# Group normalisation folded into the attention weights, and two new shares for GpSimd

## The chip, the cores and the metric

The kernel runs on one core of one Trainium2 chip. A core has five engines with queues of their own: TensorE (PE in the profile; its weight loads are listed as PEld), VectorE (DVE), ScalarE (ACT), GpSimd (POOL) and SyncE (SP, which here only issues the transfers between HBM and the on-chip memory). Each engine works through its queue in order and waits on semaphores for the others. The metric is the device time of one execution in microseconds; smaller is better.

## The reference

Input x has the shape (8, 512, 48, 48): 8 samples b, 512 channels, L = 2304 positions. Two layers follow each other, both of the form x + f(groupnorm(x)) with 32 groups of 16 channels.

Layer 0 is causal linear attention with 8 heads of 64 channels:

```python
n = groupnorm(x)
q, k, v = Wq @ n + bq, Wk @ n + bk, Wv @ n + bv
Q, K = elu(q) + 1, elu(k) + 1
den = 1 / (sum_c Q * cumsum(K) + 1e-10)
x = x + den * causal(Q, K) @ v
```

Layer 1 cuts the 512 channels into 4 scales s of 128. Each scale adds the result of the one before to its input, runs a Mamba block (a short convolution, SiLU, a projection to step, B and C, and a scan with 256 channels times 16 states), and fuses input and output by a maximum and two sigmoid weights:

```python
delta = softplus(dt @ Wdt + bdt)
h[t] = exp(delta[t] * A) * h[t - 1] + delta[t] * xs[t] * B[t]
y[t] = sum_n h[t, n] * C[t, n] + xs[t] * D
```

All of it is float32.

## The kernel before

**Two pipelines in one program.** Positions are cut into chunks of LC = 384 columns, NC = 6 to a row. Attention works on parts (b, o), o being one of four groups of 128 output channels (two heads); a part has 6 chunks, so there are 32 parts and 192 attention chunks. The second layer works on jobs (b, s, chunk), also 192, of two streams (even and odd samples) that take turns every 6 jobs. A job is 8 slots; a slot s holds 16 states times 128 channels of the scan in a tile u of 128 x 4 x 385.

**What a slot does.** u starts as the product of B (broadcast) and dxr = delta * xs. Its first LC - TAIL columns are made on DVE (`product`, L890, from a copy Bp of B in PSUM that ACT makes for two slots at a time, `inputs`, L863), the last TAIL = 152 on POOL (`last_product`, L879). ACT makes four decays exp(dr * A) in PSUM banks (L900). DVE runs four scans over u (L910). POOL multiplies all of u by C (`weigh`, L923). TensorE sums over states into yp (`gather`, L937). There are five buffers for u; POOL makes the tail of slot k+2 in slot k.

**What sets the order.** Nothing is scheduled by a compiler: Python generators (`Task`) yield a due time in half slots and the banks they need, and `beside` steps all that are due while `slot(k)` writes the instructions of slot k; the order written is the order on each engine. `ahead` writes decays up to 3 ahead of the scans (5 in two places). Six PSUM banks are shared by decays and attention. A job is 16 halves; every attention chunk takes a place 16 halves after the one before (`times`), so that in the long middle of the run each job carries one attention chunk.

**Around the change.** `statistics(b)` has DVE take batch statistics of x (L253, 24 pieces a sample) and `group_norm` makes of them norm[:, 0] = 1/std and norm[:, 1] = -mean/std per channel. `fetch` loads a chunk of 128 x 4 x 384 (tile xn) one chunk ahead. In `chunk(m)`, if o is 0, four POOL instructions (L324) scale and shift that chunk and a store keeps it as xns; parts with o from 1 to 3 load xns. `project(0)`, (1), (2) make q, k, v (L300: 4 matmuls each), `feature` applies elu + 1 with the bias of the projection (L312, L313 on ACT; L359, L367 on DVE). Later in the chunk: den by three small matmuls (L405), two DVE instructions that add 1e-10 and take the reciprocal (L433, L434), a broadcast, and the scores and outputs. `load_projections` loads the weights of the next part at the last chunk but one of a part.

In `prepare`, a job goes through the convolution (L722), SiLU on ACT (L758 to L763, between two loads of activation tables), the projection to dt, B and C (L769, L774), the step size (L782 on PE, Softplus L793 on ACT with two more table loads), dx = delta * xs on POOL (L834, two), and the transfers that spread delta, dx, B and C over partitions. `pass_on` closes a block of 6 jobs and prepares the input of the next; its POOL addition L696 makes the output of the block before, one to a chunk.

Of the kernel before, what the change touches and what calls it, by code (L numbers as in the profile page):

```python
# [9 lines left out]
F32 = mybir.dt.float32  # L10
# [7 lines left out]
P = 128  # L18
T = 128
LC = 384  # L20
NI, NQ, NGR = 4, 4, 4
SLOTS = 8
TAIL = 152
BANKS = 6
# [25 lines left out]
def attention_then_mamba_kernel(  # L50
# [64 lines left out]
    def load_scales():  # L115
# [4 lines left out]
        nc.scalar.mul(w_a, w_a, -1.0)  # L120

    power = cpool.tile([P, 4], F32, name="power")
    nc.gpsimd.memset(power, -0.5)
# [98 lines left out]

    norms, xns, x1s, done, ksums = {}, {}, {}, {}, {}

    def statistics(b):

        xv = x[b].rearrange("(t p) l -> p t l", p=P)
        stats = small.tile([P, 4, NC, 6], F32, tag="stats_a", name=f"stats_a{b}", bufs=2)
        if b == 0:

            xs = []

            def load(c):
                t = mpool.tile([P, 4, 1 + LC], F32, tag="u", name=f"xs_{c}", bufs=5)[:, :, 0:LC]
                nc.sync.dma_start(out=t, in_=xv[:, :, c * LC : (c + 1) * LC])
                xs.append(t)

            for c in range(5):
                load(c)
            load_projections()  # L240
            for c in range(NC):
                for ct in range(4):
                    nc.vector.bn_stats(stats[:, ct, c, :], xs[c][:, ct, :])
                if c == 0:
                    load(5)
                    fetch(0)
        else:
            when = begins[b] + b % 2
            for i in range(4 * NC):
                yield (when - 4, 1) if b > 1 else "1", 0  # L250
                xs = piece(b, i)
                yield (when, 1) if b > 1 else "1", 0
                nc.vector.bn_stats(stats[:, i // NC, i % NC, :], xs)  # L253
                when += PERIOD
        norms[b] = yield from group_norm(stats, 4, f"a{b}", 2)
# [9 lines left out]
    def fetch(m):  # L265

        if m == len(parts):
            return
        b, o, c = parts[m]
        if (o, c) == (0, 0):  # L270
            xns[b] = dpool.tile([512, L], F32, tag="xn", name=f"xn_{b}", bufs=B)
            x1s[b] = dpool.tile([512, L], F32, tag="x1", name=f"x1_{b}", bufs=B)
        xn = apool.tile([P, 4, LC], F32, tag="xn", name=f"xn_{b}_{o}_{c}", bufs=2)
        src = (x[b] if o == 0 else xns[b]).rearrange("(t p) l -> p t l", p=P)
        nc.sync.dma_start(out=xn, in_=src[:, :, c * LC : (c + 1) * LC])
        fetched[m] = xn

    read, passes = [0], {}

    def chunk(m):  # L280
# [16 lines left out]
        def project(j):  # L297
            ps = bank()[:, 0:LC]
            for kt in range(4):
# [6 lines left out]
                )  # L306
            return ps, bqkv_sb[:, j * 4 + o : j * 4 + o + 1]

# [6 lines left out]

        if o == 0:
            yield at(-4), 0
            while b not in norms or m not in fetched:
                yield "1w", 0
            xn, norm = fetched.pop(m), norms[b]  # L320
            for ct in range(4):
                if ct:
                    yield at(ct - 4), 0
                nc.gpsimd.tensor_scalar(  # L324
                    xn[:, ct, :],
                    xn[:, ct, :],
                    norm[:, 0, ct : ct + 1],
                    norm[:, 1, ct : ct + 1],
                    ALU.mult,
                    ALU.add,  # L330
                )
            save(xns[b].rearrange("(t p) l -> p t l", p=P)[:, :, cols], xn)
        while read[0] < m - 1:
            yield "1w", 0
        yield at(0), 1
        if o:
            xn = fetched.pop(m)
        if c == 0:
# [22 lines left out]
        yield at(2, 0), 1  # L361
        kp, kb = project(1)
        yield at(3), 0
        ex = feature(kp, kb)
        yield at(4), 0
        k = new("k", 2)
# [19 lines left out]
        nc.vector.tensor_mul(pr, q, kc)  # L386
# [15 lines left out]
        both = bank()  # L402
        den = both[:, 0 : 2 * NT]
        for i in range(NT):
            nc.tensor.matmul(den[:, 2 * i : 2 * i + 2], pr[:, subs[i]], hsel, start=True, stop=True)  # L405
        more = NT if c + 1 < NC else NT - 1
# [25 lines left out]
        rd = small.tile([P, 2 * NT], F32, tag="rd", name=f"rd_{n}", bufs=1)  # L432
        nc.vector.tensor_scalar_add(rd, den, 1e-10)  # L433
        nc.vector.reciprocal(rd, rd)  # L434
        while read[0] < m:
# [86 lines left out]
    class Stream:  # L522
# [55 lines left out]
        def pass_on(self):  # L578
# [78 lines left out]
            for c in range(NC):  # L657
# [15 lines left out]
                else:  # L673
# [29 lines left out]
    class Job:  # L703
# [6 lines left out]
        def prepare(self):  # L710
# [66 lines left out]
            save(scr, dbc[0 : 2 * NS, :])  # L777
            yield "1", 2
            vps = []
            for h in range(2):  # L780
# [4 lines left out]
                vps.append(vp)  # L785
            while spreading:
                yield "1w", 0
# [72 lines left out]
        def inputs(self, pair):  # L860

            self.Bp = psx.tile([P, 2, LC - TAIL], F32, tag="Bp", name=f"Bp_{self.n}_{pair}")
            nc.scalar.copy(self.Bp, self.B[pair % 2][:, :, 0 : LC - TAIL])  # L863

# [7 lines left out]
        def last_product(self, s):  # L872

            shape, cols = [P, NGR, TAIL], slice(LC - TAIL, LC)
# [4 lines left out]
            nc.gpsimd.tensor_tensor(  # L879
                u[:, :, 1 + LC - TAIL :],  # L880
                self.B[q // 2][:, q % 2, cols].unsqueeze(1).to_broadcast(shape),
# [5 lines left out]
        def product(self, s, u):  # L887

            shape, cols = [P, NGR, LC - TAIL], slice(0, LC - TAIL)
            nc.vector.tensor_mul(  # L890
                u[:, :, 1 : 1 + LC - TAIL],
                self.Bp[:, s % 2, :].unsqueeze(1).to_broadcast(shape),
# [264 lines left out]
    def slot(k):  # L1157
# [9 lines left out]
        elif s == 6:  # L1167
            job.gated(0)
        beside(2 * k)
        for i in range(4):  # L1170
# [41 lines left out]
    with tc.manual_schedule():  # L1212
        half_no[0] = FIRST - 6
        Task(statistics(0)).finish()
        load_scales()
        for st in streams:
# [95 lines left out]
```

## Time and profile before

| what | us |
|---|---|
| median of 3 runs (8166.18 to 8179.68) | 8173.76 |
| the profiled execution, its own time | 8173.45 |
| its span, first to last instruction | 8171.6 |
| VectorE busy | 7825.8 |
| GpSimd busy | 7747.3 |
| TensorE busy (ends modelled) | 7371.7 |
| ScalarE busy | 6974.3 |
| first scan, last scan starts at | 196, 8145 |

The page's second part shows DVE and POOL at nine tenths or more in all of the 40 slices but the first. PE's granted clock is 0.945 of full speed on average. The transfers keep the 16 DMA engines busy to seven or eight tenths, at 203 GB/s. A duration in the group list is that of one instruction by itself; on DVE and POOL the next one starts somewhat before it ends, so what an instruction costs in a full queue is the distance from its start to the next start in the timeline.

### The profile page before, as it was taken

The numbers are of one execution on the slowest core, as the hardware profiler recorded it, in microseconds if no ns is written. First come the engines' busy times: TensorE is split into PE (matmuls) and PEld (weight loads), VectorE is DVE, ScalarE is ACT, GpSimd is POOL, SyncE is SP. The second block draws the span as 40 slices with busy tenths as digits, with TensorE's granted clock in tenths as the row PEclk, the third lists the DMA queues.
The fourth block names the chain that finished last, engine by engine and source line by source line (L and its number), as shares of the span: only waits on it lengthen the run. The fifth ranks groups of instructions, "written<-read, shape, count | busy, mean of one in ns | idle before, by whom it ended". The sixth has DMA issues, their size and how long they took to land. (4 is left out here: it accounts for less than half of the span.)

```text
span 8171.6 us, 133449 instructions
## 1 busy us (share of the span) xinstructions
PE 7371.7 (90%) x39882; PEld 3532.8 (43%) x39882; DVE 7825.8 (96%) x10534; ACT 6974.3 (85%) x14914; POOL 7747.3 (95%) x3905
## 2 busy tenths in 40 slices
PE   8889999998899999999899999999988999999975
PEld 5444444444444444444444444444444444444421
DVE  3999999999999999999999999999999999999998
ACT  3888888888888888888888888888888888888876
POOL 2999999999999999999999999999999999999999
PEclk9999999999999999999999999999999999999977
DMA  6778888877787788887787788887877777777765
GB/s 199 191 189 207 210 209 212 212 199 210 200 209 204 205 212 212 207 210 201 205 216 205 200 208 209 214 211 195 212 204 204 204 204 200 204 203 199 193 172 148
DMA packets 1097351, 1655.02 MB, mean 203 GB/s; under 512 B 143913, under 2 KB 989353, under 8 KB 1096498
## 3 DMA queue, kind: packets, MB, share of 16 engines
q1 hardware_dynamic: 1096626, 1646.48, 77.8%
q8 instruction: 317, 5.19, 0.3%
q14 instruction: 408, 3.34, 0.1%
HBM read 1318.23 MB, written 327.68 MB: 201 GB/s over the span
## 5 line engine op out<-in xcount | busy, mean ns | idle before, releaser
L910 DVE TENSOR_TENSOR_SCAN u<-bank,u 128x385 f32<-128x385 f32 (+1 forms) x6144 | 5435.3, 935 | 101.6 <-ACT bank L900 101.1
L923 POOL TENSOR_TENSOR u<-u,C 128x1536 f32<-128x1536 f32 x1536 | 4894.4, 3187 | 245.4 <-DVE u L910 164.3
L900 ACT ACTIVATE bank<-dr,scales 128x385 f32<-128x385 f32 (+1 forms) x6144 | 3422.3, 579 | 617.5 <-DVE u L910 573.9
L879 POOL TENSOR_TENSOR u<-B,dxr 128x608 f32<-128x608 f32 x1536 | 2285.6, 1488 | 14.8 <-DMA B<-scr 14.8
L300 PE MATMUL bank<-xn,wq 128*128 128x384 f32 x4608 | 1862.0, 552 | 262.4 <-DVE u L910 215.6
L890 DVE TENSOR_TENSOR u<-Bp,dxr 128x928 f32<-128x928 f32 x1536 | 1682.9, 1096 | 14.9 <-DMA dxr<-xscr 7.7
L937 PE MATMUL yp<-u,cst 128*32 128x384 f32 x12288 | 1357.6, 514 | 259.7 <-POOL u L923 147.7
L300 PEld LDWEIGHTS bank<-xn,wq 128*128 128x128 f32 x4608 | 939.9, 212 | 1153.2 <-DVE u L910 360.5
L722 PE MATMUL bank<-xi,wk 128*128 128x384 f32 x3072 | 1102.4, 502 | 14.5 <-ACT xr L508 13.7
L722 PEld LDWEIGHTS bank<-xi,wk 128*128 128x128 f32 x3072 | 556.2, 191 | 568.2 <-ACT bank L900 77.3
L937 PEld LDWEIGHTS yp<-u,cst 128*32 128x32 f32 x12288 | 249.3, 109 | 904.3 <-issue 412.7
L312 ACT ACTIVATE ex<-bank,bqkv_sb 128x384 f32<-128x384 f32 x384 | 221.1, 576 | 337.0 <-PE bank L300 336.1
L900 ACT ACT_TABLE_LOAD x382 | 490.1, 1283 | 6.9
L863 ACT COPY Bp<-B 128x464 f32<-128x464 f32 x768 | 419.6, 546 | 25.7 <-DMA B<-scr 12.4
L834 POOL TENSOR_TENSOR dx<-delta,xs 128x384 f32<-128x384 f32 x384 | 385.9, 1005 | 21.6 <-ACT delta L793 21.6
L733 PE MATMUL bank<-xi,scales 128*128 128x384 f32 x768 | 325.4, 510 | 50.3 <-ACT xs L758 50.3
L955 PE MATMUL bank<-yz,scales 128*128 128x384 f32 x768 | 328.1, 534 | 37.7 <-DVE yz L949 32.8
L782 PE MATMUL bank<-dbc,steps_w 9*128 9x384 f32 x768 | 306.0, 518 | 21.8 <-DVE rd L433 12.3
L769 PE MATMUL bank<-xs,scales 128*40 128x384 f32 x768 | 285.0, 494 | 0.0
L498 PE MATMUL bank<-sm,v 128*64 128x128 f32 x2304 | 255.2, 300 | 0.0
L793 ACT ACT_TABLE_LOAD x192 | 246.3, 1283 | 3.5
L758 ACT ACT_TABLE_LOAD x192 | 246.3, 1283 | 3.5
(123 smaller groups left out, 8101.2 us busy)
## 6 DMA issues: line engine op xcount, KB each, us to landing
dr<-dscr SPq DMA_DIRECT2D x1536, 192.0 KB, 4.2
dxr<-xscr SPq DMA_DIRECT2D x1536, 192.0 KB, 4.9
xn<-xn SPq DMA_DIRECT2D x192, 768.0 KB, 5.4
B<-scr SPq DMA_DIRECT2D x1536, 96.0 KB, 4.2
C<-scr SPq DMA_DIRECT2D x1536, 96.0 KB, 2.7
dscr<-delta SPq DMA_DIRECT2D x192, 384.0 KB, 5.2
xscr<-dx SPq DMA_DIRECT2D x192, 384.0 KB, 2.9
xn<-in_x SPq DMA_DIRECT2D x48, 768.0 KB, 5.3
```

The costliest lines, as they stand in the source:

```text
L300: nc.tensor.matmul(ps, wqs[m // NC][:, kt, j * P : (j + 1) * P], xn[:, kt, :], start=(kt == 0), stop=(kt == 3),)
L722: nc.tensor.matmul(xc, wk[:, k, h * P : (h + 1) * P], xi[:, c0 + k : c0 + k + LC], start=(k == 0), stop=(k == 3),)
L733: nc.tensor.matmul(zp, w_gate[:, s, h * P : (h + 1) * P], xi[:, c0 + 3 : c0 + 3 + LC], start=True, stop=True,)
L834: nc.gpsimd.tensor_tensor(dx[:, h, :], delta[:, h, :], xs[:, h, :], ALU.mult)
L863: nc.scalar.copy(self.Bp, self.B[pair % 2][:, :, 0 : LC - TAIL])
L879: nc.gpsimd.tensor_tensor(u[:, :, 1 + LC - TAIL :], self.B[q // 2][:, q % 2, cols].unsqueeze(1).to_broadcast(shape), self.dxr[h][:, :, col ...
L890: nc.vector.tensor_mul(u[:, :, 1 : 1 + LC - TAIL], self.Bp[:, s % 2, :].unsqueeze(1).to_broadcast(shape), self.dxr[s // NQ][:, :, cols],)
L900: nc.scalar.activation(dA[:, cols], self.dr[h][:, g, cols], AF.Exp, scale=w_a[:, self.w[1], NGR * h + g, q : q + 1],)
L910: nc.vector.tensor_tensor_scan(u[:, g, cols], dA[:, cols], u[:, g, cols], 0.0, ALU.mult, ALU.add,)
L923: nc.gpsimd.tensor_tensor(u[:, :, 0:LC], u[:, :, 1:], self.C[q // 2][:, q % 2, :].unsqueeze(1).to_broadcast([P, NGR, LC]), ALU.mult,)
L937: nc.tensor.matmul(self.yp[g * 32 : g * 32 + 32, 0:LC], state_sum, u[:, g, 0:LC], start=False, stop=s % NQ == NQ - 1, skip_group_check=True,)
L955: nc.tensor.matmul(self.xm[:, 0:LC], w_out[:, self.w[1], h, :], self.yz[:, h, :], start=(h == 0), stop=(h == 1),)
```

## The change

- The normalisation of attention's input leaves POOL. x itself is projected by every part; the weights are scaled by 1/std on ACT (`scaled`, four instructions of 128 x 384 a part, in place), and the shift goes into the bias: `shifts` multiplies the unscaled weights by -mean/std on PE (12 matmuls with one column a part, into three unused columns, 384 to 386, of the bank that holds k's projection), `shifted` adds the layer's bias on ACT (three instructions of 128 x 1). For the next part all this is done in the last chunk of the part before; for the first part in `adapt`, ahead of everything.
- The copy xns and its 48 stores are gone.
- The 1e-10 of the denominator comes from a matmul of the identity with a constant tile, ahead of the three of den; DVE takes the reciprocal straight from PSUM.
- POOL's share of the product is 128 columns in slots 0 and 1 of a job and 174 in slots 2 to 7.
- POOL's addition of `pass_on` moves to a place 17 halves ahead of the job (slot 7 in place of slot 4); the step-size matmuls L782 are written one half later, together with their Softplus; in slot 1 the gather that waits is written ahead of the other work.
- Statistics of samples 4 to 7 start earlier, with one piece every second job for each of two samples.

```diff
-TAIL = 152
+WIDE, TAIL = 128, 174
...
+    tiny = cpool.tile([P, 2 * LC // T], F32, name="tiny")
+    nc.gpsimd.memset(tiny, 1e-10)
...
-            when = begins[b] + b % 2
+            when, gap = begins[b] + (b % 2 if b < 4 else 0), PERIOD if b < 4 else 2 * PERIOD
...
-                when += PERIOD
+                when += gap
...
-        src = (x[b] if o == 0 else xns[b]).rearrange("(t p) l -> p t l", p=P)
+        src = x[b].rearrange("(t p) l -> p t l", p=P)
...
+    def shifts(i, to):
+        w, norm = wqs[i], norms[parts[i * NC][0]]
+        for j in range(3):
+            for kt in range(4):
+                nc.tensor.matmul(
+                    to[:, j : j + 1],
+                    w[:, kt, j * P : (j + 1) * P],
+                    norm[:, 1, kt : kt + 1],
+                    start=(kt == 0),
+                    stop=(kt == 3),
+                    skip_group_check=True,
+                )
+
+    def shifted(i, shift):
+        o = parts[i * NC][1]
+        biases[i] = bias = small.tile([P, 3], F32, tag="bias", name=f"bias_{i}", bufs=2)
+        for j in range(3):
+            nc.scalar.activation(
+                bias[:, j : j + 1],
+                shift[:, j : j + 1],
+                AF.Identity,
+                bias=bqkv_sb[:, j * 4 + o : j * 4 + o + 1],
+            )
+
+    def scaled(i, kt):
+        w, norm = wqs[i], norms[parts[i * NC][0]]
+        nc.scalar.activation(w[:, kt, :], w[:, kt, :], AF.Copy, scale=norm[:, 0, kt : kt + 1])
...
-            return ps, bqkv_sb[:, j * 4 + o : j * 4 + o + 1]
+            return ps, biases[m // NC][:, j : j + 1]
...
-            for ct in range(4):
-                if ct:
-                    yield at(ct - 4), 0
-                nc.gpsimd.tensor_scalar(
...
-            save(xns[b].rearrange("(t p) l -> p t l", p=P)[:, :, cols], xn)
...
         kp, kb = project(1)
+        ahead_of = m // NC + 1 if c == NC - 1 and m + 1 < len(parts) else None
+        if ahead_of is not None:
+            extra = bank.held[-1][:, LC : LC + 3]
+            shifts(ahead_of, extra)
         yield at(3), 0
         ex = feature(kp, kb)
+        if ahead_of is not None:
+            shifted(ahead_of, extra)
...
+        if ahead_of is not None:
+            scaled(ahead_of, 0)
         yield at(6), 0
+        if ahead_of is not None:
+            scaled(ahead_of, 1)
...
         yield at(7), 0
+        if ahead_of is not None:
+            scaled(ahead_of, 2)
...
+        yield at(8), 0
+        if ahead_of is not None:
+            scaled(ahead_of, 3)
...
+        nc.tensor.matmul(den, ident, tiny, start=True, stop=False, skip_group_check=True)
...
-        nc.vector.tensor_scalar_add(rd, den, 1e-10)
-        nc.vector.reciprocal(rd, rd)
+        nc.vector.reciprocal(rd, den)
...
+                    yield (first - 17, 1) if not last else "1", 0
                     nc.gpsimd.tensor_tensor(xa, xa, fu, ALU.add)
...
-            yield "1", 2
+            while spreading:
+                yield "1w", 0
+            spreading.append(n)
+            yield "2", 2
             vps = []
...
-            while spreading:
-                yield "1w", 0
-            spreading.append(n)
-            yield "1", 0
             delta = mpool.tile([P, 2, LC], F32, tag="delta", name=f"delta_{n}", bufs=1)
...
+            width = LC - (TAIL if pair else WIDE)
...
+            tail = TAIL if s > 1 else WIDE
...
+        if b > 3:
+            begins[b] -= (4 * NC - b % 2) * PERIOD
...
+        if s == 1 and len(waiting) > 1:
+            waiting.pop(0)()
         beside(2 * k)
```

More of the change, by code (lines that the diff above doesn't have):

```diff
@@ L219, in group_norm @@
         return norm
-    norms, xns, x1s, done, ksums = {}, {}, {}, {}, {}
+    norms, x1s, done, ksums = {}, {}, {}, {}
     def statistics(b):
@@ L270, in fetch, with adapt @@
         if (o, c) == (0, 0):
-            xns[b] = dpool.tile([512, L], F32, tag="xn", name=f"xn_{b}", bufs=B)
             x1s[b] = dpool.tile([512, L], F32, tag="x1", name=f"x1_{b}", bufs=B)
         xn = apool.tile([P, 4, LC], F32, tag="xn", name=f"xn_{b}_{o}_{c}", bufs=2)
-        src = (x[b] if o == 0 else xns[b]).rearrange("(t p) l -> p t l", p=P)
+        src = x[b].rearrange("(t p) l -> p t l", p=P)
         nc.sync.dma_start(out=xn, in_=src[:, :, c * LC : (c + 1) * LC])
         fetched[m] = xn
-    read, passes = [0], {}
+    read, passes, biases = [0], {}, {}
+    def shifts(i, to):
[23 more added lines that the diff above has]
+        nc.scalar.activation(w[:, kt, :], w[:, kt, :], AF.Copy, scale=norm[:, 0, kt : kt + 1])
+    def adapt():
+        bank = Banks()
+        yield FIRST - 6, 1
+        while 0 not in norms:
+            yield "1w", 1
+        shift = bank()
+        shifts(0, shift)
+        shifted(0, shift)
+        bank.free()
+        for kt in range(4):
+            scaled(0, kt)
     def chunk(m):
@@ L314, in feature @@
             return ex
-        if o == 0:
-            yield at(-4), 0
-            while b not in norms or m not in fetched:
-                yield "1w", 0
-            xn, norm = fetched.pop(m), norms[b]
-            for ct in range(4):
-                if ct:
-                    yield at(ct - 4), 0
[L324 to L331, printed above, removed]
-            save(xns[b].rearrange("(t p) l -> p t l", p=P)[:, :, cols], xn)
+        while m not in fetched:
+            yield "1w", 0
         while read[0] < m - 1:
@@ L335, in chunk @@
         yield at(0), 1
-        if o:
-            xn = fetched.pop(m)
+        xn = fetched.pop(m)
+        assert m // NC in biases
         if c == 0:
@@ L403, in chunk @@
         den = both[:, 0 : 2 * NT]
+        nc.tensor.matmul(den, ident, tiny, start=True, stop=False, skip_group_check=True)
         for i in range(NT):
-            nc.tensor.matmul(den[:, 2 * i : 2 * i + 2], pr[:, subs[i]], hsel, start=True, stop=True)
+            nc.tensor.matmul(
+                den[:, 2 * i : 2 * i + 2],
+                pr[:, subs[i]],
+                hsel,
+                start=False,
+                stop=True,
+                skip_group_check=True,
+            )
         more = NT if c + 1 < NC else NT - 1
@@ L777, in prepare @@
             save(scr, dbc[0 : 2 * NS, :])
-            yield "1", 2
+            while spreading:
+                yield "1w", 0
+            spreading.append(n)
+            yield "2", 2
             vps = []
@@ L785, in prepare @@
                 vps.append(vp)
-            while spreading:
-                yield "1w", 0
-            spreading.append(n)
-            yield "1", 0
             delta = mpool.tile([P, 2, LC], F32, tag="delta", name=f"delta_{n}", bufs=1)
@@ L860, in inputs @@
         def inputs(self, pair):
-            self.Bp = psx.tile([P, 2, LC - TAIL], F32, tag="Bp", name=f"Bp_{self.n}_{pair}")
-            nc.scalar.copy(self.Bp, self.B[pair % 2][:, :, 0 : LC - TAIL])
+            width = LC - (TAIL if pair else WIDE)
+            Bp = psx.tile([P, 512], F32, tag="Bp", name=f"Bp_{self.n}_{pair}")
+            self.Bp = Bp[:, 0 : 2 * width].rearrange("p (f l) -> p f l", f=2)
+            nc.scalar.copy(self.Bp, self.B[pair % 2][:, :, 0:width])
         def skip(self, h):
@@ L872, in last_product @@
         def last_product(self, s):
-            shape, cols = [P, NGR, TAIL], slice(LC - TAIL, LC)
+            tail = TAIL if s > 1 else WIDE
+            shape, cols = [P, NGR, tail], slice(LC - tail, LC)
             h, q = s // NQ, s % NQ
@@ L879, in last_product @@
             nc.gpsimd.tensor_tensor(
-                u[:, :, 1 + LC - TAIL :],
+                u[:, :, 1 + LC - tail :],
                 self.B[q // 2][:, q % 2, cols].unsqueeze(1).to_broadcast(shape),
@@ L887, in product @@
         def product(self, s, u):
-            shape, cols = [P, NGR, LC - TAIL], slice(0, LC - TAIL)
+            width = LC - (TAIL if s > 1 else WIDE)
+            shape, cols = [P, NGR, width], slice(0, width)
             nc.vector.tensor_mul(
-                u[:, :, 1 : 1 + LC - TAIL],
+                u[:, :, 1 : 1 + width],
                 self.Bp[:, s % 2, :].unsqueeze(1).to_broadcast(shape),
@@ L1214, in attention_then_mamba_kernel @@
         Task(statistics(0)).finish()
+        Task(adapt()).finish()
         load_scales()
```

## The prediction

> **What bounds the kernel now.** I read the busy times first, then the busy time by stretches of six jobs, then the waits inside a stretch, then the timeline.
>
> ```profile
> span 8171.6 us, 133449 instructions
> PE 7371.7 (90%) x39882; PEld 3532.8 (43%) x39882; DVE 7825.8 (96%) x10534; ACT 6974.3 (85%) x14914; POOL 7747.3 (95%) x3905
> ```
>
> DVE and POOL are within 78 us of each other, so no sum over the run tells which one bounds. The stretches do:
>
> ```profile
> 2692.00:2937.00 245.00, 226.39 (x1251) 109.37 (x1246) 241.84 (x326) 218.46 (x469) 237.57 (x115) 0.97 0.80 207
> 3930.00:4189.00 259.00, 230.08 (x1218) 109.52 (x1220) 245.34 (x331) 218.34 (x467) 253.18 (x140) 0.94 0.78 204
> 7173.00:7418.00 245.00, 224.28 (x1252) 108.27 (x1251) 238.88 (x320) 216.55 (x466) 237.75 (x115) 0.99 0.77 201
> 7908.00:8150.00 242.00, 147.15 (x580) 47.77 (x580) 226.40 (x266) 170.57 (x371) 237.96 (x117) 0.72 0.63 154
> ```
>
> Each line is six jobs: start and end, length, then busy time (and count) of PE, PEld, DVE, ACT and POOL. An ordinary job takes 245/6 = 40.9 us, with six pieces of statistics (first line) or none (third). The second line holds parts with o = 0: 24 normalising instructions more on POOL, POOL 98% busy, 43.2 us a job. The last has no attention left, and there POOL runs without any gap from 7990 to 8150: 40.3 us a job. So two things set the pace. In an ordinary stretch DVE does, at 97.5%, and what it lacks to 100% is in the next two views, of 7173 to 7418 (sum of us, times, longest) and of the last slot of one job:
>
> ```profile
> DVE u L910 <- ACT bank L900: 5.8, 7, 0.9
> POOL u L923 <- DVE u L910: 5.3, 5, 1.5
> ```
>
> ```profile
> 7207.85 1.28 ACT L758 ACT_TABLE_LOAD   x1
> ...
> 7209.87 1.09 DVE L890 TENSOR_TENSOR u<-Bp,dxr 128x928 f32<-128x928 f32 x1
> ...
> 7211.24 1.28 ACT L900 ACT_TABLE_LOAD   x1
> 7211.35 0.93 DVE L910 TENSOR_TENSOR_SCAN u<-bank,u 128x384 f32<-128x384 f32 x1
> ...
> 7213.15 2.66 DVE L910 TENSOR_TENSOR_SCAN u<-bank,u 128x384 f32<-128x384 f32 x3 [0.87 <-ACT bank L900]
> ...
> 7214.25 3.19 POOL L923 TENSOR_TENSOR u<-u,C 128x1536 f32<-128x1536 f32 x1 [1.49 <-DVE u L910]
> ```
>
> Once a job ACT makes no decays from 7207.85 to 12.54, because of SiLU and its tables; DVE runs out (0.87), and POOL, which had caught up, waits behind it (1.49). I call it the hole. The first and third stretch differ by 3 us of DVE work and not in length: a bit of DVE work next to the hole is free. In the o = 0 stretch POOL decides.
>
> **The change part by part.** Prices are distances from start to start. The rows:
>
> ```profile
> L324 POOL TENSOR_SCALAR xn<-xn,norm_a 128x384 f32<-128x384 f32 x192 | 128.0, 669 | 74.5 <-DMA xn<-in_x 45.8 <-PE bank L300 28.3 <-DVE norm_a L211 0.4
> L433 DVE TENSOR_SCALAR rd<-bank 128x6 f32<-128x6 f32 x192 | 27.2, 141 | 21.4 <-PE bank L423 21.4
> L879 POOL TENSOR_TENSOR u<-B,dxr 128x608 f32<-128x608 f32 x1536 | 2285.6, 1488 | 14.8 <-DMA B<-scr 14.8
> L890 DVE TENSOR_TENSOR u<-Bp,dxr 128x928 f32<-128x928 f32 x1536 | 1682.9, 1096 | 14.9 <-DMA dxr<-xscr 7.7 <-ACT Bp L863 7.2
> ```
>
> *DVE.* The product of 928 elements costs 1.02 us (7209.87 to 7210.89), a multiply of 384 elements 0.46 (L386, 7238.77 to 7239.23), so 1.03 ns an element. Slots 2 to 7 get 840 elements: 6 x 88 x 1.03 = 0.54 us a job less. Slots 0 and 1 get 1024: 2 x 0.10 more, but both products run in slot 7, in the hole, where 0.87 us are idle. L433 goes (7215.73 to 7215.90, 0.17). Outside the hole: 0.71 us a job less, 40.9 to 40.2.
>
> *POOL.* weigh (1536 elements) costs 3.13, the tail (608) 1.44, dx (384) 0.95. That gives 1.82 ns an element between the two large ones, 2.19 between the two small ones. 512 and 696 elements, two and six times a job: 6 x 88 - 2 x 96 = 336 elements, +0.61 us at 1.82, +0.74 at 2.19; I take 1.82, the larger pair having the same broadcast shape. Without the o = 0 work an ordinary job has POOL busy 237.75/6 = 39.6; it becomes 40.2 (40.4). The normalisation, 0.63 a piece (3933.69 to 3934.32), goes: 192 x 0.63 = 121 us, against 192 x 0.61 = 117 us added. POOL's total stands still; it is spread evenly.
>
> [...]
>
> *An ordinary job after.* DVE 40.2, POOL 40.2. Two engines of equal length that hand work to each other lose something; between nothing (POOL without a gap for 160 us at the end) and the 1.2 us of POOL's idle time in an ordinary job now. I take 0.3: 40.5 us. The lag fits: POOL's heavier tails lie in slots 0 to 5, where DVE carries the attention work, its light ones and the moved addition (0.95) in slots 6 and 7, just ahead of the hole in which POOL idled 1.49.
>
> *The end of a part, 31 times.* The 12 one-column matmuls cost what L405's cost, 0.73 us for 6 records or three matmuls: 2.9 us on PE, between k's projection and the scores (L457). From 0, if ACT gets past, to 12 x 0.38 = 4.6 by a single matmul of the statistics (L202, 144.03). In the last-chunk job they run here:
>
> ```profile
> 7226.83 2.85 PE L300 MATMUL bank<-xn,wq 128*128 128x384 f32 x8
> ...
> 7229.72 0.58 ACT L312 ACTIVATE ex<-bank,bqkv_sb 128x384 f32<-128x384 f32 x1 [1.11 <-PE bank L300]
> ...
> 7231.60 1.79 DVE L910 TENSOR_TENSOR_SCAN u<-bank,u 128x385 f32<-128x385 f32 x2
> ```
>
> ACT does k's two features until 7230.66 and then stands before the three biases: 2.9 - 1.0 = 1.9 us of waiting and 3 x 0.2 (L591) of work, 2.5 us late. Queued behind them are the decays of 7230.66. The first is ready at 7231.24 and is needed by the second scan of the pair at 7231.60, which starts at 7232.45: 1.2 us of cover. DVE loses 2.5 - 1.2 = 1.3 us; bounds 0 and 4.6 - 1.0 + 0.6 - 1.2 = 3.0. PE's own 2.9 us are taken from idle time (224.28 of 245 busy, 3.4 us a job) before the next convolution. POOL, equal in length, runs on through half of it: 0.65 x 31 = 20 us; bounds 0 and 93. The four scalings on ACT, 0.59 each (L868), fall in slots 5 to 7, where ACT waits for DVE 0.95 (7234.36) and 0.26 at a time and idles 28 of 245 us in all: nothing; with that cover gone, 2.4 x 31 = 74 us.
>
> *Small edits, at nothing.* The den matmul on PE (0.25 a job) is covered by PE's idle 3.4. Bp copies lose 21 elements on average. L782 moves behind the gather that waits for POOL's weigh of the last slot; it ends then about 0.6 us ahead of its Softplus (7220.49), after 1.3 us of table load. If POOL lags 1 us more there, 0.4 us of every job is lost: 77 us, in the range only. The moved L696 takes its store on SP along. SP loses 48 stores, which it waited on for 190 us in 42 waits behind L324; loads of x replace loads of the copy, same size. Statistics keep their count of 168; by the first stretch above they are nearly free when thinly spread.
>
> *The stretches that were longer.* Scans run 7954 us, 192 x 40.9 is 7853, so 101 lie above. The o = 0 stretches (six jobs at 43.2 to 43.6 and twelve beside them at 41.6 to 42.5, three times) hold 72 of them, which go; 29 stay (the group norms of samples, the first jobs).
>
> *Start and end.* 196 us before the first scan, PE without gaps from 70 on. `adapt` adds 2.9 + 0.6 + 2.4 us in a row, about 3 beyond what POOL's first pieces cost; later chunks no longer wait for POOL and its store (PE and its weight loads waited 126 us for L324, here and in the o = 0 stretches). I take -4, bounds -15 and +8. The end stays 22.
>
> **Sum.** 192 x 40.5 = 7776, + 20 + 29 + 192 + 22 = 8039 span. The profiled execution lies 1.9 above its span and 0.3 under the median of the runs: 8041 us, 132 (1.6%) less.
>
> **The rivals.**
> 1. *The hole, not DVE's sum, sets the job.* What DVE saves turns up as more waiting for ACT, which is solidly busy from 7212 to 7229. For it: the two stretches of different DVE work and equal length. Against it: the stretch at 7664 to 7908 has 0.4 us less DVE work a job and is 0.2 us a job shorter. Job 40.9: 7853 + 20 + 29 + 214 = 8116, 8118 with the 2 us around the span.
> 2. *POOL becomes the bound and keeps its idle time.* The 1.49 us wait stays in every job as in five of six now, and POOL cannot lag because the step size now waits for its gather. 40.2 + 1.2 = 41.4: 7949 + 20 + 29 + 214 = 8212, 8214 in the end: slower. It decides from 41.2 a job on. Against it: the gapless 160 us.
> 3. *The ends of parts cost in full*: DVE's 93 and ACT's 74 us in place of 20, 8188, less the 0.3 us a job allowed for two equal engines, since POOL then has room (58): 8130. For it: ACT is solidly busy where the biases come; against it: two features that already run while PE works.
> 4. *No friction, and the start gains*: 40.25 a job, 0 for the parts: 7728 + 29 + 185 + 22 = 7964, 7966.
>
> **How the numbers follow.** Forecast (8000 to 8085) 0.50; the hole 0.15; parts in full 0.10; no friction 0.12; POOL with its idle time 0.08; in between, no gain, 0.05. Under 0.2% (16 us) a measurement of this kernel can't tell from none. Faster 0.87, same 0.05, slower 0.08. Range 7970 to 8140: it leaves out the slower cases, half of no gain, and the edge of case 4.
>
> **What would show it.** The o = 0 stretches vanish: all stretches of six jobs 243 to 246 us. POOL about 99% busy in the middle, its waits for L910 mostly gone; the product rows of 840 elements 1.00 us and 1024 about 1.19, the tails 1.31 and 1.65. A wait of ACT for the one-column matmuls of about 2 us, 31 times. It is wrong if DVE's wait for decays grows past 1.5 us a job, if POOL idles 1 us a job or more, or if TensorE's granted clock falls with the added matmuls.

## The result, and the profile after

The changed kernel takes 8266.27 us (median of 4 runs, 8259.60 to 8290.52) against 8169.97 (4 runs of the kernel before beside it): 1.0123 times as long, 95% interval 1.0110 to 1.0136. The forecast was 8041 us, the range 7970 to 8140; both were wrong, and so was the sign.

The page of the changed kernel, span and busy times:

```profile
span 8257.8 us, 135309 instructions
...
PE 7504.3 (91%) x41034; PEld 3691.7 (45%) x41034; DVE 7752.6 (94%) x10342; ACT 7015.1 (85%) x15138; POOL 7765.7 (94%) x3714
```

VectorE lost 73 us of work, as it should, and the span grew by 86. GpSimd's total stood still (+18) and its share of the span fell to 94%: neither of the two engines that set the pace before fills more of the span. The time is in waits of VectorE. The stretches of six jobs that answer to the four shown before (start and end, length, busy time and count of PE, PEld, DVE, ACT and POOL, TensorE's granted clock, share of the DMA engines, GB/s):

```profile
2712.00:2962.00 250.00, 233.45 (x1291) 115.82 (x1290) 240.37 (x320) 220.05 (x476) 242.40 (x116) 0.96 0.75 204
3971.00:4222.00 251.00, 235.50 (x1248) 114.83 (x1248) 240.14 (x327) 218.03 (x471) 238.44 (x114) 0.93 0.72 194
7239.00:7488.00 249.00, 232.45 (x1285) 114.94 (x1281) 236.66 (x313) 217.38 (x472) 241.24 (x115) 0.96 0.73 197
7985.00:8230.00 245.00, 149.18 (x556) 50.56 (x556) 218.91 (x263) 170.54 (x371) 236.18 (x115) 0.71 0.59 152
```

The second one no longer stands out (259 us before): the stretches with o = 0 are gone, as forecast. But the ordinary ones rose from 245 to 249 and 250, and in them VectorE is busy 95 to 96%, where it was 97.5 to 98.7 in the ordinary ones before. The waits of VectorE (us in all, times, longest), of the changed kernel:

```profile
DVE k L399 <- ACT bias L298: 95.1, 31, 5.3
DVE q L498 <- PE bank L493: 85.9, 83, 4.4
DVE u L962 <- ACT bank L952: 79.8, 149, 4.3
```

and the two of the kernel before that stand in the same places:

```profile
DVE u L910 <- ACT bank L900: 101.1, 131, 2.9
DVE q L450 <- PE bank L445: 44.5, 59, 5.9
```

The first line is new: once at the end of each part, k. The second has nearly doubled. The third has become smaller in all, but it has moved. Sorting the gaps between VectorE's instructions by slot shows where: they add up to 348 us in place of 192, with 60 in slot 1 (9 before), 92 in slot 2 (58), 95 in slot 3 (1) and 79 in slot 7 (108). The hole in slot 7 is indeed filled better by the wide products, as forecast.

**Loss A, the end of a part.** The timeline of the changed kernel, in one of the 31 jobs (start, duration, engine, line; in brackets the idle time before it, and what ended it):

```profile
4570.79 2.85 PE L341 MATMUL bank<-xn,wq 128*128 128x384 f32 x8
...
4573.08 1.80 DVE L962 TENSOR_TENSOR_SCAN u<-bank,u 128x385 f32<-128x385 f32 x2
...
4573.47 2.73 PE L285 MATMUL bank<-norm_a,wq 128*128 128x1 f32 x24
...
4576.24 0.58 ACT L353 ACTIVATE ex<-bank,bias 128x384 f32<-128x384 f32 x1 [3.73 <-PE bank L285]
4576.72 0.55 ACT L354 ACTIVATE bank<-bank,bias 128x384 f32<-128x384 f32 x1
4577.30 0.56 ACT L298 ACTIVATE bias<-bank,bqkv_sb 128x1 f32<-128x1 f32 x3
...
4577.90 0.56 DVE L399 SCALAR_TENSOR_TENSOR k<-ex,bank 128x384 f32<-128x384 f32 x1 [3.02 <-ACT bias L298]
```

k's projection is done at 4573.6. ScalarE's features, which read none of the three new columns, start at 4576.24, when the last of the 12 one-column matmuls is done. The prediction had ScalarE run both features in that time. The semaphores in the trace say why it can't: in the 31 last chunks of parts no record of k's projection raises one, the last of the 24 one-column records raises the only one, and that is the one for which the first feature waits. In every other chunk the projection's own last record raises it. So the wait stands in the program's order of signals, and not in what the chip does with columns of one bank. VectorE waits 3.02 us, not 1.3, with k ahead of the next scans in its queue; slot 3 of these jobs takes 7.92 us on average (middle of the run), 4.90 before.

**Loss B, slots 1 and 2.** The step-size matmuls (L834) now stand behind the gather that waits for GpSimd. One job of the changed kernel, TensorE and the end of the chain on VectorE:

```profile
4556.90 0.85 PE L989 MATMUL yp<-u,cst 128*32 128x384 f32 x8
4559.84 0.85 PE L989 MATMUL yp<-u,cst 128*32 128x384 f32 x8 [2.08 <-POOL u L975]
4560.62 2.43 PE L834 MATMUL bank<-dbc,steps_w 9*128 9x384 f32 x4
4562.99 5.31 PE L341 MATMUL bank<-xn,wq 128*128 128x384 f32 x8
4568.13 0.49 PE L493 MATMUL bank<-cst,rdb 128*128 128x128 f32 x3
...
4568.66 0.55 DVE L498 TENSOR_TENSOR q<-q,bank 128x384 f32<-128x384 f32 x1 [1.28 <-PE bank L493]
```

TensorE waits 2.08 us with nothing to do, and then the step size, q's projection and the three transposes for VectorE's q stand in a row. The busy times and the granted clock (the column after the five engines) around it:

```profile
4556.00:4560.00 4.00, 1.92 (x37) 1.09 (x40) 4.00 (x6) 4.00 (x12) 4.00 (x3) 1.00 0.50 140
4560.00:4564.00 4.00, 4.00 (x14) 1.55 (x7) 4.00 (x6) 3.48 (x6) 4.00 (x2) 0.64 1.02 251
4564.00:4568.00 4.00, 4.00 (x7) 2.04 (x7) 2.93 (x4) 2.67 (x6) 4.00 (x3) 0.50 1.03 308
4568.00:4572.00 4.00, 3.91 (x20) 1.90 (x19) 3.15 (x6) 3.67 (x10) 3.90 (x3) 1.00 0.81 284
```

After the idle stretch the mean granted clock of the windows is 0.64 and then 0.50, and q's eight records take 5.31 us, where k's eight in the job of loss A took 2.85. Over the run, matmuls of L834 above 600 ns are 324 of 768; of L782 before, 25. Before, the step size was followed by the gather in 190 of 192 jobs; now q's projection follows it in 184. TensorE's wait for GpSimd at the gather rose from 147.7 us in 185 to 393.2 in 206.

In slot 1 it is ScalarE that passes the delay on. Its Softplus (L841) and the table load ahead of it now wait for the step size, which they did nowhere in the kernel before, and the decays that VectorE's scans need stand behind them in its queue. VectorE waits for a scan 66 times in slot 1, 56 us in all, and each of these waits ends within 0.15 us of the end of a decay.

```profile
ACT delta L841 <- PE bank L834: 48.7, 77, 2.5
ACT L841 <- PE bank L834: 35.3, 30, 3.7
```

### The profile page after: what moved, and what is told of

It reads as the page before. It is cut to its first block, busy times and chain, and to the rows that moved or that the text cites. A ratio compares the mean times of both kernels' runs of the same rounds, so it can differ in the third digit from the quotient of the medians.

```text
span 8257.8 us, 135309 instructions
## 1 busy us (share of the span) xinstructions
PE 7504.3 (91%) x41034; PEld 3691.7 (45%) x41034; DVE 7752.6 (94%) x10342; ACT 7015.1 (85%) x15138; POOL 7765.7 (94%) x3714
## 5 line engine op out<-in xcount | busy, mean ns | idle before, releaser
L930 POOL TENSOR_TENSOR u<-B,dxr 128x696 f32<-128x696 f32 (+1 forms) x1536 | 2430.8, 1583 | 16.5 <-DMA ksum<-before 12.1
L989 PE MATMUL yp<-u,cst 128*32 128x384 f32 x12288 | 1352.6, 513 | 560.7 <-POOL u L975 393.2
L341 PE MATMUL bank<-xn,wq 128*128 128x384 f32 x4608 | 1834.0, 547 | 11.3 <-DVE u L962 5.7
L942 DVE TENSOR_TENSOR u<-Bp,dxr 128x840 f32<-128x840 f32 (+1 forms) x1536 | 1616.8, 1053 | 12.2 <-ACT Bp L913 7.2
L353 ACT ACTIVATE ex<-bank,bias 128x384 f32<-128x384 f32 x384 | 221.0, 576 | 452.0 <-PE bank L341 335.4
L913 ACT COPY Bp<-B 128x420 f32<-128x420 f32 (+1 forms) x768 | 406.2, 529 | 27.2 <-DMA B<-scr 13.6
L834 PE MATMUL bank<-dbc,steps_w 9*128 9x384 f32 x768 | 401.1, 654 | 1.9 <-ACT S L485 1.9
L782 PE MATMUL bank<-xi,scales 128*128 128x384 f32 x768 | 306.6, 500 | 27.0 <-ACT xs L807 24.1
L1007 PE MATMUL bank<-yz,scales 128*128 128x384 f32 x768 | 307.1, 517 | 25.0 <-DVE yz L1001 17.8
L834 PEld LDWEIGHTS bank<-dbc,steps_w 9*128 9x128 f32 x768 | 158.8, 228 | 210.8 <-ACT bank L952 85.7
```

The costliest lines, as they stand in the source:

```text
L341: nc.tensor.matmul(ps, wqs[m // NC][:, kt, j * P : (j + 1) * P], xn[:, kt, :], start=(kt == 0), stop=(kt == 3),)
L834: nc.tensor.matmul(vp, steps_w[32:41, s, h * P : (h + 1) * P], dbc[32:41, :], start=True, stop=True)
L913: nc.scalar.copy(self.Bp, self.B[pair % 2][:, :, 0:width])
L930: nc.gpsimd.tensor_tensor(u[:, :, 1 + LC - tail :], self.B[q // 2][:, q % 2, cols].unsqueeze(1).to_broadcast(shape), self.dxr[h][:, :, col ...
L942: nc.vector.tensor_mul(u[:, :, 1 : 1 + width], self.Bp[:, s % 2, :].unsqueeze(1).to_broadcast(shape), self.dxr[s // NQ][:, :, cols],)
L989: nc.tensor.matmul(self.yp[g * 32 : g * 32 + 32, 0:LC], state_sum, u[:, g, 0:LC], start=False, stop=s % NQ == NQ - 1, skip_group_check=True,)
```

## The experiments

Each kernel was timed against the kernel before on the same chip, whose median lay between 8170.8 and 8178.8. "Changed" is the kernel after the change. Where two runs are compared, the difference is that of their ratios times 8171 us; with half-widths of 0.0010 to 0.0017 it is good to some 18 us either way.

**The shift in v's bank.** The 12 matmuls, the biases and the scalings move from behind k's projection to behind v's.

```diff
-        if ahead_of is not None:
-            extra = bank.held[-1][:, LC : LC + 3]
-            shifts(ahead_of, extra)
         yield at(3), 0
         ex = feature(kp, kb)
-        if ahead_of is not None:
-            shifted(ahead_of, extra)
...
         vp, vb = project(2)
+        if ahead_of is not None:
+            extra = bank.held[-1][:, LC : LC + 3]
+            shifts(ahead_of, extra)
```

> The changed kernel, with the twelve one-column matmuls, the three biases and the four scalings moved: into spare columns of v's bank, behind v's projection, the biases behind vT. Theory A (k's feature stands before the matmuls because it reads the same bank): the 90 us that DVE waits for k at the ends of parts go, and some 10 behind them; about 8266 - 100 = 8166 us, ratio to before 1.000. Rival (TensorE lacks these 3 us a part wherever they stand): DVE waits as much elsewhere; ratio 1.009 or more.

8256.63 us, ratio 1.0102 (1.0085 to 1.0119). The theory fell: the wait for k is gone, and another one has come, here in the waits of VectorE in this run:

```profile
DVE pr L421 <- ACT before L415: 80.7, 29, 7.3
...
DVE pr L421 <- PE bank L405: 17.0, 7, 3.7
```

pr needs the running sum of k, and its matmul stands behind the 12 in TensorE's queue. VectorE's gaps fell by 90 us in slot 3 and rose by 66 in slot 4. So which bank they use is hardly the point. In both places TensorE is busy with them for 2.7 us while something that VectorE needs soon stands behind them; a place with nothing urgent behind it was not tried.

**The old order, whole and in half.** The first of three runs takes back L834's place and the early gather of slot 1, the second does so together with the shift in v's bank, the third takes back L834's place alone.

```diff
-            while spreading:
-                yield "1w", 0
-            spreading.append(n)
-            yield "2", 2
+            yield "1", 2
             vps = []
...
+            while spreading:
+                yield "1w", 0
+            spreading.append(n)
+            yield "1", 0
             delta = mpool.tile([P, 2, LC], F32, tag="delta", name=f"delta_{n}", bufs=1)
...
-        if s == 1 and len(waiting) > 1:
-            waiting.pop(0)()
```

> The changed kernel with the step-size matmuls and the gather of slot 1 back in their old places. Theory B (the step size now stands behind a gather that waits for GpSimd): DVE's 58 us of waiting for decays in slot 1 go, and of the 88 us around q in slot 2 some 30; about 8180 us, ratio 1.001. Rival (GpSimd's larger share makes the gathers late, whatever the order): gain under 20 us, ratio 1.010 or more.

> Both edits at once. If A and B hold and add: 8266 - 190 = 8076 us, ratio 0.988, an ordinary job 39.8 to 40.2 us. Rival: GpSimd, with 40.3 us of work a job, becomes the bound and holds it at 40.7 a job or more: 8130 or more, ratio 0.995.

> The changed kernel with the step-size matmuls alone back in their old place; the gather of slot 1 stays early. Theory B1 (their place behind the gather is the cost): most of what e2 gains, 60 to 90 us, ratio about 1.002. Rival B2 (the early gather is the cost: TensorE stands idle before it): under a third of that, ratio 1.009 or more.

8216.14 us, 1.0047 (1.0032 to 1.0062); with the shift in v's bank as well 8211.99, 1.0042 (1.0027 to 1.0057), no difference; L834 alone 8213.97, 1.0043 (1.0028 to 1.0058). It is L834's place, and the early gather costs nothing. VectorE's gaps in slots 1 and 2 went from 151 to 15 us. That should have been worth more than the 65 us between 1.0123 and 1.0043, and VectorE's busy time tells why: it rose from 7752.6 to 7817.3. The group that grew, in the changed kernel and in the run with L834 alone (elements and count, then busy us and mean ns of one):

```profile
L641 DVE TENSOR_SCALAR wt<-wt 128x2 f32<-128x2 f32 x32 | 29.8, 932 | 0.3 <-ACT wt L639 0.3
```

```profile
L641 DVE TENSOR_SCALAR wt<-wt 128x2 f32<-128x2 f32 x32 | 109.7, 3428 | 0.3 <-ACT wt L639 0.3
```

An addition of two elements takes 3.43 us. In the timeline of that run it ends with GpSimd's instruction, not with its own work:

```profile
2960.95 3.20 POOL L976 TENSOR_TENSOR u<-u,C 128x1536 f32<-128x1536 f32 x1
...
2962.46 4.28 DVE L641 TENSOR_SCALAR wt<-wt 128x2 f32<-128x2 f32 x1
...
2964.09 1.00 POOL L883 TENSOR_TENSOR dx<-delta,xs 128x384 f32<-128x384 f32 x1
2965.05 1.66 POOL L931 TENSOR_TENSOR u<-B,dxr 128x696 f32<-128x696 f32 x1
2968.78 3.19 POOL L976 TENSOR_TENSOR u<-u,C 128x1536 f32<-128x1536 f32 x1 [2.07 <-DVE u L963]
```

It starts at 2962.46 beside GpSimd's L976, does not come in at 2964.15 when that ends, nor after dx, and ends at 2966.74, 0.03 us after L931. And it ends where GpSimd runs out of work that is ready: the next L976 needs scans that stand behind the addition in VectorE's queue. In 21 of the 32 times the addition outlasts three or more GpSimd instructions, and GpSimd stands idle for 2.07 us each time right after it. In the changed kernel this addition mostly starts 0.3 or 1.2 us before a GpSimd instruction ends and gets in at that end; three are held for longer. This price depends on the moment. The kernel before had it too: five of its 32 additions took 2.77 to 5.77 us, the others 0.17 to 0.41, but no row there could tell how many the change would hold.

**The addition on ScalarE.** As L834 alone, with

```diff
-                nc.vector.tensor_scalar_add(wt[:, 0:2], wt[:, 0:2], 1.0)
+                nc.scalar.activation(wt[:, 0:2], wt[:, 0:2], AF.Copy, bias=1.0)
```

> The changed kernel with the step-size matmuls back in their old place (as in the run before that one, 8214 us) and the addition of 1 in pass_on (L641, 128x2) moved from VectorE to ScalarE. Theory: on VectorE this addition of two elements is held until GpSimd's running instruction ends (0.93 us a time in the changed kernel, 3.43 us with the old order, 110 us in 32); on ScalarE it costs about 0.2 us and VectorE only waits some 0.3 us for it. 8214 less 80 to 110: 8104 to 8134 us; slot 3 of the jobs after a block's end falls from 8.7 back under 5.9 us. Rival: something else that is late in the same place holds VectorE there (the input of the next block, or ScalarE itself), and the time stays at 8200 or above.

8119.03 us, 0.9945 (0.9928 to 0.9962): 80 us less, as the theory had it, and faster than before for the first time. The slot in which pass_on's addition falls went from 8.42 to 5.37 us on average. The same job as in loss B, in this run:

```profile
4488.65 1.55 PE L831 MATMUL bank<-dbc,steps_w 9*128 9x384 f32 x4
4491.00 1.51 PE L990 MATMUL yp<-u,cst 128*32 128x384 f32 x8 [0.80 <-POOL u L976]
4492.44 3.75 PE L341 MATMUL bank<-xn,wq 128*128 128x384 f32 x8
4496.02 0.49 PE L493 MATMUL bank<-cst,rdb 128*128 128x128 f32 x3
```

The step size runs in the time in which TensorE waits for GpSimd, and the idle stretch is 0.80 us, not 2.08. VectorE's q starts at 4497.81, with no wait.

**The mean as a 385th column.** As the run before, without the 12 matmuls. The scaled weights times -mean are the shift, so -mean stands as column 384 of the first chunk of a part, whose three projections are 385 wide; ScalarE takes the bias from the last column.

```diff
+    def column(m):
+        nc.scalar.copy(fetched[m][:, :, LC], norms[parts[m][0]][:, 1, :])
...
+            width = LC + 1 if c == 0 else LC
...
-                    ps,
+                    whole[:, 0:width],
...
-                    xn[:, kt, :],
+                    xn[:, kt, 0:width],
...
+            if c == 0:
+                nc.scalar.activation(
+                    bias,
+                    whole[:, LC : LC + 1],
+                    AF.Identity,
+                    bias=bqkv_sb[:, j * 4 + o : j * 4 + o + 1],
+                )
...
+        if n == 4:
+            nc.scalar.mul(norm[:, 1, :], gm[:, 0, :], -1.0)
+            return norm
```

> As e7, and the 12 one-column matmuls at the end of a part are gone: the mean stands as a 385th column beside the first chunk's x (one ScalarE copy of 128x4 a part), each projection of that chunk is 385 wide, and its last column gives the shift; ScalarE adds the layer's bias there, three instructions a part as before. Theory: PE's 2.7 to 3 us at the end of a part are what VectorE waits for, at k or at what stands behind it (92 us in the runs so far): e7 less 75 to 95 us, 8015 to 8055 us, and no slot of 7.9 us left in the jobs where a part ends. Rival: the scalings of the weights or the first chunk's own dependence on them take as much: the wait moves to the first chunk's q, and the time falls by less than 30 us.

8023.92 us, 0.9826 (0.9811 to 0.9841): 97 us less. No slot of 7.9 us is left (slot 3 of those jobs takes 4.80, like that of any other). Not all of the 97 lies at the ends of parts. The two profiled executions differ by 87 us: 13 ahead of the first scan, which moves from 207.5 to 194.7, and 75 between the first and the last. The edit also takes 64 scalings of 128x1 in group_norm off VectorE, busy 8.4 us in the changed kernel. The rival holds for a little of it: with ScalarE's bias now ahead of the first chunk's features, VectorE waits 16.2 us before k in 24 first chunks, where the changed kernel has 4.3 in 2. Its page and its stretches:

```profile
span 8024.6 us, 133950 instructions
...
PE 7341.0 (91%) x40266; PEld 3567.7 (44%) x40266; DVE 7705.0 (96%) x10246; ACT 7034.4 (88%) x15210; POOL 7754.7 (97%) x3714
```

```profile
2644.00:2886.00 242.00, 227.54 (x1264) 111.49 (x1264) 239.20 (x319) 220.12 (x477) 241.46 (x116) 0.97 0.80 210
3866.00:4109.00 243.00, 229.32 (x1234) 110.83 (x1235) 239.20 (x318) 219.25 (x475) 238.33 (x115) 0.94 0.76 200
7029.00:7271.00 242.00, 227.78 (x1268) 112.05 (x1267) 236.88 (x314) 219.20 (x475) 242.00 (x116) 0.97 0.78 204
```

These are the 243 us a stretch, and the GpSimd at 98% and more, that the prediction expected of the changed kernel.

**Controls on the kernel before.** The addition on ScalarE alone, the two shares alone, and both.

```diff
-TAIL = 152
+WIDE, TAIL = 128, 174
...
+            width = LC - (TAIL if pair else WIDE)
...
+            tail = TAIL if s > 1 else WIDE
```

> The kernel before with only that addition on ScalarE. Theory: there it takes VectorE 29.7 us in 32 (0.93 each, 0.17 when nothing holds it): 20 to 28 us less, 8150 to 8160 us. Rival: it hides there and nothing changes (within 8 us).

> The kernel before with only the two shares of GpSimd, 128 and 174 columns; the normalisation stays on GpSimd, with its stores. The prediction's reasons: VectorE loses 0.54 us a job outside the hole, and GpSimd gains 0.61 us, which it has in ordinary jobs (busy 39.6 of 40.9) but not in the 48 or so jobs that also normalise (43 us each): 144 x 0.5 = 72 us less, 48 x 0.6 = 29 us more, 8130 to 8140 us. Rival: GpSimd keeps its wait of 1.2 us in every job and becomes the bound, 41.4 us a job and over 43.5 where it normalises: 8200 to 8260 us.

> The kernel before with the two shares, and the addition of 1 on ScalarE. With the shares alone VectorE's addition took 104 us in 32 (3.25 each, 0.93 before), and the time rose to 8211. Theory: this addition is what made the shares alone slower: 8211 less 80 to 100, 8110 to 8130 us, below the kernel before with the addition on ScalarE (8152). Rival: GpSimd is the bound (busy 7882 us with the shares alone, against 7747) and VectorE only waits elsewhere: 8180 us or more.

The addition alone: 8152.28 us, 0.9978 (0.9969 to 0.9988), 18 us less, just under the 20 to 28 expected. The shares alone: 8211.47, 1.0056 (1.0041 to 1.0071), slower, with 79.5 us in the addition where 29.7 had been. (The 104 in the last expectation took the median, 3.25, for the mean; the mean is 2.49.) Both: 8141.22, 0.9960 (0.9946 to 0.9974). So the held addition is what made the shares alone slower: with it on ScalarE in both, they gain 15 us, which the uncertainty nearly covers. That is less than the 43 (72 less 29) of the expectation: VectorE's gaps in slot 2 rose from 54 to 97 us. GpSimd, which still normalises there, is busy 7884.6 of 8137.5 us.

**The price of L834's place, without the addition.** The changed kernel with only the addition on ScalarE.

> The changed kernel with only the addition of 1 in pass_on on ScalarE; the step-size matmuls stay behind the gather. Against the run that also has them back (8119 us) this gives the price of their place without the addition that hid part of it. Theory: VectorE's waits in slots 1 and 2 (58 us on decays, some 30 us on q) and what follows them cost 100 to 130 us: 8220 to 8250 us. Rival: the place of the step-size matmuls is worth only the 52 us that the run with the old place showed: 8165 to 8180 us, and the addition's 80 us came from elsewhere.

8265.45 us, 1.0111 (1.0096 to 1.0126): no different from the changed kernel, and 136 us above the run that also has L834 in its old place. VectorE's gaps account for it: 67 and 96 us in slots 1 and 2, against 3 and 11.

**The shares, given the rest.** The run with the 385th column, with 152 columns in all slots.

```diff
-WIDE, TAIL = 128, 174
+WIDE, TAIL = 152, 152
```

> The fastest run so far (8024 us: mean as a 385th column, step-size matmuls in their old place, addition on ScalarE) with GpSimd's share at 152 columns in all slots, as before the change. Theory: the prediction's reason for the shares holds: VectorE gets 88 elements more in each of six slots of a job, 0.54 us, and an undisturbed job goes from 39.8 to 40.3: 80 to 105 us more, 8104 to 8129 us. Rival: VectorE and GpSimd are equally long and hand work to each other, so that a lighter GpSimd gives back what VectorE gets: within 30 us of 8024.

8074.66 us, 0.9882 (0.9867 to 0.9897): the shares are worth 46 us, between the theory and its rival. Slots 0 to 5 (distance from one slot's first scan to the next one's, medians over the middle of the run) fall from 29.91 to 29.44 us with the new shares, 0.47 where 0.54 was priced. Slots 6 and 7 rise from 10.31 to 10.42: the hole does not take all of the wider products, and VectorE's gaps in slot 6 rise from 11 to 36 us; the product's wait for the transfer of dxr, 12.2 us in 7 with 152 columns, is 32.9 in 34.

**The best.** The run with the 385th column, with group_norm's variance of x made by 128x1 instructions whose scalars come from a tile, and the reciprocal of pass_on half a slot behind ScalarE's addition.

```diff
-            nc.vector.tensor_mul(gm[:, 2, :], gm[:, 1, :], gm[:, 1, :])
-            nc.vector.tensor_add(gm[:, 2, :], gm[:, 2, :], mv[:, :, 1])
+        for ct in range(n):
+            dif = gm[:, 1, ct : ct + 1]
+            nc.vector.tensor_scalar(
+                gm[:, 2, ct : ct + 1], dif, dif, mv[:, ct, 1:2], ALU.mult, ALU.add
+            )
...
+                yield "1", 0
                 nc.vector.reciprocal(wt[:, 0:2], wt[:, 0:2])
```

> The fastest run so far with two more edits of the kind that its trace points to: group_norm's variance term for the 4-column case is made by four instructions of 128x1 with scalars from a tile (273 ns each in the trace) in place of a multiplication and an addition of 128x4, of which the addition is held by GpSimd (2.6 us and 0.87 us, 8 times each); and the reciprocal in pass_on is written half a slot after ScalarE's addition, for which VectorE waits 0.44 us, 30 times. Theory: 16 to 20 us and 10 to 13 us less: 7992 to 8000 us. Rival: VectorE has to wait for GpSimd there anyway: 8015 to 8030 us.

8001.82 us (7991.81 to 8008.95), 0.9791 (0.9776 to 0.9805): 29 us under the run with the 385th column, faster than both kernels, 2.1% under the one before. VectorE's wait ahead of pass_on's reciprocal, 13.8 us in 31 with the 385th column, is 0.5 in one. The group of the new instructions, in this run:

```profile
L197 DVE TENSOR_SCALAR gm_a<-gm_a,mv_a 128x1 f32<-128x1 f32 x32 | 6.5, 267 | 0.3
```

6.5 us in place of 27.9 (20.9 and 7.0 in the changed kernel).

## Why the prediction was wrong

The runs give the change as a sum, each term the difference of two ratios times 8171 us:

| step | from, to | us |
|---|---|---|
| addition off VectorE | before, 0.9978 | -18 |
| normalisation in weights, by the 385th column, and the small edits without L834's place | 0.9978, 0.9882 | -78 |
| the shares | 0.9882, 0.9826 | -46 |
| the shift by 12 matmuls at the end of a part | 0.9826, 0.9945 | +97 |
| L834 behind the gather | 0.9945, 1.0111 | +136 |
| addition back on VectorE, in this order | 1.0111, 1.0123 | +10 |

Each term is good to some 18 us, so the last is no different from nothing. The second holds several edits that no run takes apart. The fourth holds the start and the scalings of group_norm as well, as said above.

*"Ordinary job after 40.5"* was right in kind. The slots that nothing disturbs add up to 39.87 us in the run with the 385th column against 40.58 before, 0.7 less; I had named 0.7 for VectorE outside the hole, and 0.3 of friction with it. Slots 0 to 5 gave more (30.27 to 29.44), the hole took back 0.1. The changed kernel itself does not get there: 249 and 250 us for six jobs are 41.5 and 41.7 a job, and GpSimd idles 1.3 us in each, which is one of the signs that the prediction had named for being wrong.

*"POOL's total stands still, spread evenly"*: 7747.3 to 7765.7 us, and the o = 0 stretches are gone. Right. In the tails 145 us of busy time were added (2285.6 to 2430.8), 139 from start to start, where I had 117. The slope between the two small instructions, 2.19 ns an element, gives 0.74 us a job, 142 in all, and would have come closer than the 1.82 that I took.

*"Small edits at nothing"* is the first step that failed. It priced L782's move by the slack at its end, 0.6 us ahead of Softplus, and left TensorE's queue out of it. Before, the step size filled the time in which TensorE waits for GpSimd. Behind the gather it leaves that time empty and is added to the row that follows: step size, q's projection, the transposes for VectorE's q. At the half clock that follows the empty time the step size is itself slower: its mean granted clock is below 0.75 in 90 of 192 jobs of the changed kernel, in 6 before, and its four records take 2.92 us where that clock is below 0.60 and 1.55 where it is above 0.99 (medians). q's projection meets it no more often than before: it ran at a mean granted clock below 0.75 in 101 of 192 chunks before and in 97 after. 136 us in place of nothing, and above the 77 that the range had for it. Rival 2 named this dependence, "the step size now waits for its gather", but with GpSimd as the bound at 41.4 us a job; its 8214 was the nearest of the rivals, for another reason.

*"The end of a part"* is the second. It had ScalarE do k's two features beside the 12 matmuls, half of the rest absorbed by GpSimd, 20 us. The features wait for the matmuls, and VectorE for the features, some 3.0 us each time: 95.1 us of wait in 31. In the time it is 97 with the start, 75 between the first and the last scan, so little is absorbed. Rival 3, "ends of parts in full", had VectorE's part of this term nearly right, 93; the 74 that it added for ScalarE did not come. The run in v's bank showed that the dependence of the features is not the root: without it 66 of 90 us of gaps came back behind the running sum of k, whose matmul then stands behind the 12 in TensorE's queue. That TensorE idles 3.4 us a job says nothing on whether it idles here. A version with the features written ahead of the matmuls, so that k's projection raises its own semaphore, wasn't tried.

*The four scalings, "nothing"*, held nearly: in the run with the 385th column they are still there, and slot 4 of those jobs takes 5.01 us in place of 4.80, 6 us in 31. *The start* was -4 by forecast; the first scan moved from 196 to 203 us in the changed kernel and to 195 with the 385th column. The six other kernels with the 12 matmuls lie between 202.5 and 207.5, so these and their biases seem to take more than the 3 us given to them.

*What no step had*: VectorE's addition in pass_on. In the changed kernel moving it changes nothing, but with L834 in its old place it costs 80 us. Only with all three out of the way does the measured time, 8024, come near the predicted 8041, and that nearness is in part luck. The gains are 78 and 46 us, 124 together, where the forecast had 77 for the shorter job, 72 for the o = 0 stretches and 4 at the start, 153 in all. The 18 of the addition, which nobody forecast, and the 20 that the forecast set aside for the ends of parts and that this run does not pay make up for it.

## What to carry to other kernels

An in-order engine that is not the bottleneck still has places where its time is dear: before an instruction is put into its queue, read what stands directly behind it there and who waits for that, not how long the engine idles on average. An instruction moved from inside a wait to behind it can cost time: here 136 us in 192 jobs, 0.7 us a job, of the 1.55 to 2.43 us that the two matmuls take. And when a change has saved work and the time has risen, split it with both signs in mind: here two losses of 97 and 136 us lay over gains of 78 and 46, and a third of 80 showed only when one of them was gone.

## What the runs showed of the hardware

*A tiny instruction on VectorE can be held for several GpSimd instructions.* The addition of a constant to 128x2 elements took 0.17 us at its shortest and 7.03 at its longest (medians 0.35 in the changed kernel, 4.29 with L834 in its old place), and in 31 of the changed kernel's 32, as in the one at 2962.46, it ended 0.02 to 0.03 us after a GpSimd instruction; the last of the 32 took 0.17, with no GpSimd instruction running. The reciprocal of the same two elements never took more than 0.17, and the 128x1 instructions with scalars from a tile (L655, L658) no more than 0.28. The addition can outlast the GpSimd instruction beside which it starts: at 2964.15 that one had finished, and VectorE got in only after two more. In each of the 21 long cases it got in when GpSimd had nothing ready to start, and in 19 of them GpSimd was by then waiting for VectorE's scan.

*TensorE's clock can fall after a short wait.* In the windows of loss B it is granted 1.00, then 0.64 and 0.50 (means) after a wait of 2.08 us and 1.92 busy us in 4. Nor does it take a wait of 2.08 us. From 400 us to 500 us before the end the clock falls 109 times in the kernel before and 103 times in the changed one; the longest pause of matmuls in the 3.41 us ahead of a fall (the shortest stretch at half clock in either trace) has a median of 0.65 us there and 1.90 here, and is at most 3.32 and 2.96. What decides is not shown. The kernel before has as many such stretches, so it isn't their number but what stands behind them that costs.
